# Own-row transposes of a graph-attention layer, emitted later behind their gather

## The chip, the cores and the metric

The kernel runs on one core of one Trainium2 chip. The metric is the device time of one launch in microseconds (us), the median of three runs.

## The reference

Eight batches of 2048 nodes with 256 channels pass through two graph-attention layers that share one symmetric, sparse adjacency matrix (a node has between a few and 38 neighbours, itself among them). Layer 0 is this; layer 1 has four heads, additive scores and an elu in its place:

```python
h1 = einsum('bnc,cd->bnd', inp, W1)
h2 = einsum('bnc,cd->bnd', inp, W2)
h3 = einsum('bnc,cd->bnd', inp, W3)
e = einsum('bnd,bmd->bnm', h1, h2)
e = where(adj > 0, leaky_relu(e, 0.2), NEG_INF)
h_prime = einsum('bnm,bmd->bnd', softmax(e), h3)
x = layernorm(x + relu(h_prime))
```

## The kernel before, in words

**Sparse form.** A set-up sorts the nodes by their number of neighbours and cuts them into 16 tiles of 128 rows. Each tile t has SLOTS[t] slots (38 down to 12), and a slot holds one neighbour of each of its 128 rows. A **unit** is one layer, one half of the batches (4 of 8, so a row is 1024 numbers) and one tile. Layer 0 has 32 units: half 0 with the tiles from the fewest slots to the most, then half 1 likewise. With W1 and W2 multiplied beforehand into A, a score is the product of g (own row times A) with the neighbour's raw row, so only raw rows are gathered.

**Four parts of a unit in layer 0.**
- `before0` (L503): an indirect DMA on POOL gathers the unit's own rows into xo (L505; xo has two buffers), four DMAs on SP copy them to xr for the residual (L509), TensorE transposes xo in two groups of four (L515, through `transposed`, L403), ScalarE copies each group into xT (L405), TensorE multiplies by A (L413), and ScalarE evicts the two halves into g (L520). Then the unit is marked ready.
- `logits0` (L524): VectorE multiplies every gathered row with g and sums it (L540), 4 batches a slot; then come leaky relu, mask, exp and the division by the sum.
- `sums0` (L620): ScalarE scales each gathered row by its weight in place (L631), and TensorE adds the slot to accumulators in PSUM by identity matmuls (L609, `add_slot`; the profile counts 8 matmuls a slot). The add frees the slot's ring tile.
- `after0` (L659): ScalarE evicts the sums into hs (L644), TensorE transposes hs and multiplies by W3, VectorE adds the residual and takes statistics, ScalarE normalises y (L393), TensorE transposes y into x1T and makes the projection q for layer 1 (L693), which POOL scatters to a table in HBM (L197).

**The ring.** Gathered neighbours come in chunks of two slots into a ring of 16 tiles (32 slots), shared by all units. `pump` (L461) issues a chunk's gathers as soon as a credit is there; `sums0` gives the credit back when it emits the last add of a chunk, and on the chip the gather waits until that add is done.

**What sets the order.** A driver written in Python emits everything in **ticks** (L901). In each, `sums` has just emitted one slot; then `tick` pumps gathers, lets the score stream run up to two steps while it is less than a limit ahead, and moves the first generator of each of three queues, starts (`before0`), ends (`after0`) and lists:

```python
for queue in queues:
    for _ in range(min(len(queue), 2)):
        if queue and next(queue[0], queue) is queue:
            queue.popleft()
clock[0] += 1
```

Only the head of a queue moves, so a start that takes longer holds the ones behind it. The start of unit j + 3 is queued when at most half of unit j's slots are left to add (L934); the first three units are queued at the beginning. POOL's instructions keep the order of emission (L337). The other engines' are ordered by the planner of the language, which takes emission as priority and may put a later instruction first where an earlier one isn't ready in its own estimate. `before0` counts its distance from gather to transposes with four bare `yield`s (L512). LATE is 6, and `clock[0]` is the number of the tick.

Of the kernel before, what the change touches and what calls it, by code (L numbers as in the profile page):

```python
# [40 lines left out]
LATE = 6  # L41
# [82 lines left out]
def fast_path(  # L124
# [59 lines left out]
    def wide_tile(name):  # L184
        return wp.tile([P, 2 * QW], F32, tag="t", name=name)

    def gather(dst, table, index):

        nc.gpsimd.indirect_dma_start(  # L189
            out=dst, out_offset=None, in_=table, in_offset=AT(ap=index, axis=0),  # L190
            bounds_check=table.shape[0] - 1, oob_is_err=False,
        )
# [205 lines left out]
    def transposed(src, name, dst):  # L398

        for i in range(2):  # L400
            pt = ps_tile(f"ps_t_{name}_{i}")
            for j in range(4):
                nc.tensor.transpose(pt[:, ts(j, P)], src[:, ts(4 * i + j, P)], ident)  # L403
            yield
            nc.scalar.copy(dst[:, ts(i, 512)], pt)  # L405
        yield

    def projected(srcT, weight, name, evict):
        for i in range(2):
            pp = ps_tile(f"ps_p_{name}_{i}")  # L410
            for j in range(2):
                for k in range(KC):
                    nc.tensor.matmul(  # L413
                        pp[:, ts(j, C)],
                        lhsT=srcT[:, ts((2 * i + j) * KC + k, P)],
                        rhs=weight[:, k, :],
                        start=(k == 0),
                        stop=(k == KC - 1),
                    )
            yield  # L420
            evict(i, pp)
        yield
# [23 lines left out]
    clock = [0]  # L446
# [56 lines left out]
    def before0(u):  # L503
        xo = xop.tile([P, HC], F32, tag="xo", name=f"xo_{u.name}")
        gather(xo, xg[u.h][:, :], order[:, u.t : u.t + 1])  # L505
        u.xr = xrp.tile([P, 2, HW], F32, tag="xr", name=f"xr_{u.name}")
        for r in range(2):
            for c in range(2):
                nc.sync.dma_start(  # L509
                    u.xr[64 * c : 64 * c + 64, r, :], xo[64 * r : 64 * r + 64, ts(c, HW)]  # L510
                )
        for _ in range(4):  # L512
            yield
        xT = wide_tile(f"xT_{u.name}")
        yield from transposed(xo, f"x_{u.name}", xT)  # L515
        while scored[0] < u.index - 1:
            yield
        u.g = gp.tile([P, HC], F32, tag="g", name=f"g_{u.name}")
        yield from projected(
            xT, w.A, f"g_{u.name}", lambda i, pp: nc.scalar.copy(u.g[:, ts(i, 512)], pp)  # L520
        )
        u.ready = True
# [357 lines left out]
    for j, u in enumerate(units):  # L880
        u.index = j
    before = (before0, before1)
    logits = (logits0, logits1)
    sums = (sums0, sums1)
# [354 lines left out]
```

## Time and profile before

| | us |
|---|---|
| median of three runs | 2752.31 (2752.2 to 2755.29) |
| the profiled execution's own time | 2757.27 |
| its span, first to last instruction | 2755.5 |
| busy: VectorE / TensorE / POOL / ScalarE | 2358.9 / 1884.3 / 1509.5 / 1475.2 |
| TensorE waiting for xo at the transposes (L403) | 165.1, 27 times |
| VectorE waiting for gathered chunks at L540 | 135.9 |
| first and last transposes of own rows, start | 120.5 and 1535.2 |

Layer 0 takes the span up to about 1720 us, layer 1 the rest. In the profile's rows a group is named by line, engine, operation and the tiles it writes and reads (out<-in); x and a number is a count, and what stands behind an arrow in brackets is what ended the idle time just before. A tile of the ring appears as s, a table of raw rows in HBM as xg.

### The profile page before, as it was taken

What the parts mean: (1) busy time and instruction counts of PE and PEld (TensorE: products, weight loads), DVE (VectorE), ACT (ScalarE), POOL (GpSimd) and SP (SyncE); (2) the same over time, 40 slices, a digit from 0 to 9 for tenths busy, and PEclk for the clock granted to TensorE, in tenths of its full rate; (3) what the DMA queues carried; (4) which work ended last, traced back from release to release, by engine and by line L of the source; (5) the groups of instructions that cost most, each with busy time, mean ns of one, the idle gap of its engine ahead of it and who ended that gap; (6) DMA issues with size and microseconds to landing.
All of it is one profiled execution on the core that took longest, in us unless ns stands there. A gap on an engine that the chain in (4) does not pass through costs nothing. (4 is left out here: it accounts for less than half of the span.)

```text
span 2755.5 us, 41008 instructions
## 1 busy us (share of the span) xinstructions
PE 1884.3 (68%) x12003; PEld 788.4 (29%) x12003; DVE 2358.9 (86%) x7255; ACT 1475.2 (54%) x3465; POOL 1509.5 (55%) x1506
## 2 busy tenths in 40 slices
PE   0148888888776767676878677766566576675663
PEld 0123434333333334343333322311122112121221
DVE  7679999999987875777787786799999899999996
ACT  6137777878779986868788779221111111210212
POOL 1354454545444543544544455577767777775772
PEclk9569899999898888898888888878878888877886
DMA  9996776868674665767776765799789999986991
GB/s 388 386 374 216 263 278 226 281 227 274 233 244 168 212 218 197 262 215 254 234 263 229 257 223 193 272 337 351 270 313 352 329 335 335 361 312 254 340 337 66
DMA packets 248024, 749.41 MB, mean 272 GB/s; under 512 B 55712, under 2 KB 73248, under 8 KB 241648
## 3 DMA queue, kind: packets, MB, share of 16 engines
q0 software_dynamic: 192064, 644.32, 66.2%
q1 hardware_dynamic: 54464, 101.21, 10.3%
q8 instruction: 98, 1.61, 0.2%
q10 hardware_dynamic: 1264, 1.18, 0.1%
q14 instruction: 134, 1.10, 0.1%
HBM read 721.50 MB, written 84.48 MB: 292 GB/s over the span
## 5 line engine op out<-in xcount | busy, mean ns | idle before, releaser
L609 PE MATMUL acc<-s,ident 64*64 64x512 f32 x9632 | 1363.4, 659 | 448.5 <-issue 226.6
L540 DVE CUSTOM_DVE_ANT_0 j<-s,g 128x256 bf16<-128x256 f32 x2408 | 1019.5, 423 | 201.5 <-DMA s<-xg,idx 135.9
L189 POOL DMA_INDIRECT s<-xg,idx x602 | 631.0, 1048 | 769.0 <-ACT s L631 283.5
L631 ACT ACTIVATE s<-s,e 128x256 f32<-128x256 f32 x2408 | 999.2, 503 | 27.3 <-DVE e L566 26.5
L189 POOL DMA_INDIRECT s<-qg,idx x602 | 610.6, 1014 | 249.9 <-issue 123.8
L609 PEld LDWEIGHTS acc<-s,ident 64*64 64x64 f32 x9632 | 386.5, 145 | 1219.2 <-issue 675.6
L793 DVE TENSOR_TENSOR s<-s,p 128x2048 f32<-128x2048 f32 (+1 forms) x312 | 682.0, 2201 | 0.8 <-issue 0.2
L381 ACT ACTIVATE z<-mv,roots 128x4 f32<-128x4 f32 x64 | 18.9, 296 | 509.7 <-DVE mv L371 509.6
L540 DVE DVE_READ_ACCUMULATOR2_ANT e<- 128x1 f32 x2408 | 196.0, 81 | 0.0
L693 PE MATMUL ps_q<-wqs,x1T 128*128 128x264 f32 x512 | 147.4, 425 | 37.2 <-ACT x1T L405 25.9
L197 POOL DMA_INDIRECT out_dram<-o,oidx x128 | 129.9, 1015 | 75.2 <-ACT o L393 40.1
L403 PE MATMUL ps_t_x<-ident,xo 128*128 128x128 f32 x256 | 56.6, 364 | 165.1 <-DMA xo<-xg,order 165.1
L393 ACT ACTIVATE o<-xr,nmr,rstd 128x256 f32<-128x256 f32 x128 | 66.4, 589 | 134.1 <-DVE nmr L389 102.2
L413 PE MATMUL ps_p_g<-A,xT 128*128 128x256 f32 x512 | 129.8, 400 | 9.5 <-DVE so L702 5.5
L413 PE MATMUL ps_p_h<-w_sb,hT 128*128 128x256 f32 x512 | 127.8, 392 | 1.5 <-ACT hT L405 1.5
L693 PEld LDWEIGHTS ps_q<-wqs,x1T 128*128 128x128 f32 x512 | 100.5, 206 | 88.9 <-ACT x1T L405 31.2
L413 PEld LDWEIGHTS ps_p_g<-A,xT 128*128 128x128 f32 x512 | 97.1, 197 | 53.8 <-DVE so L702 9.0
L488 DVE MAX8 m<-nb 128x8 f32<-128x2048 f32 x44 | 100.5, 2285 | 13.3 <-DMA nb<-edges,order 13.2
L413 PEld LDWEIGHTS ps_p_h<-w_sb,hT 128*128 128x128 f32 x512 | 92.1, 190 | 63.3 <-issue 19.5
L760 ACT ACTIVATE e<-e 128x304 f32<-128x304 f32 (+11 forms) x34 | 14.9, 439 | 175.7 <-DVE e L759 175.6
L403 PEld LDWEIGHTS ps_t_x<-ident,xo 128*128 128x128 f32 x256 | 37.9, 184 | 232.9 <-issue 219.0
L393 ACT ACTIVATE y<-y,nmr,rstd 128x256 f32<-128x256 f32 x128 | 67.2, 589 | 32.1 <-DVE nmr L389 31.8
(128 smaller groups left out, 1426.6 us busy)
## 6 DMA issues: line engine op xcount, KB each, us to landing
adj<-in_adj_dram SPq DMA_DIRECT2D x16, 1024.0 KB, 8.9
edges<-adj SPq DMA_DIRECT2D x16, 1024.0 KB, 19.7
xr<-xo SPq DMA_DIRECT2D x128, 128.0 KB, 6.7
x1s<-y SPq DMA_DIRECT2D x32, 512.0 KB, 7.4
xr<-x1s SPq DMA_DIRECT2D x32, 512.0 KB, 6.9
s<-xg,idx POOLq DMA_INDIRECT x602
s<-qg,idx POOLq DMA_INDIRECT x602
xg<-in_x_dram SPq DMA_DIRECT2D x4, 2048.0 KB
```

Of the source, the lines that this page charges most:

```text
L189: nc.gpsimd.indirect_dma_start(out=dst, out_offset=None, in_=table, in_offset=AT(ap=index, axis=0), bounds_check=table.shape[0] - 1, oob_i ...
L197: ins = nc.gpsimd.indirect_dma_start(out=table, out_offset=AT(ap=index, axis=0), in_=src, in_offset=None)
L381: nc.scalar.activation(z, mv[:, :, 1], AF.Ln, bias=w.roots[:, 0:1])
L393: nc.scalar.activation(dst[:, b, :], y[:, b, :], AF.Identity, bias=nmr[:, b : b + 1], scale=rstd[:, b : b + 1],)
L403: nc.tensor.transpose(pt[:, ts(j, P)], src[:, ts(4 * i + j, P)], ident)
L413: nc.tensor.matmul(pp[:, ts(j, C)], lhsT=srcT[:, ts((2 * i + j) * KC + k, P)], rhs=weight[:, k, :], start=(k == 0), stop=(k == KC - 1),)
L488: nc.vector.max(m[:, ts(i, 8)], v)
L540: nc.vector.tensor_tensor_reduce(out=jt, in0=rows[:, s, ts(b, C)], in1=u.g[:, ts(b, C)], scale=1.0, scalar=0.0, op0=ALU.mult, op1=ALU.add, ...
L609: nc.tensor.matmul(acc[r][64 * c : 64 * c + 64, :], lhsT=ident[rr, rr], rhs=rows[rr, s, c * 2 * w_ : (c + 1) * 2 * w_].rearrange("p (j w) ...
L631: nc.scalar.activation(v, v, AF.Copy, scale=u.p[i][:, b, k : k + 1])
L693: nc.tensor.matmul(pq[:, : C + 2 * H], lhsT=x1T[:, ts(i * KC + k, P)], rhs=w.wqs[:, k, :], start=(k == 0), stop=(k == KC - 1),)
L793: nc.vector.tensor_tensor(v, v, pv.unsqueeze(3).to_broadcast([P, n * HB, H, D]), ALU.mult)
```

## The change

The four bare yields between the gather of own rows and their transposes are replaced by a wait on the driver's clock: eight ticks after the gather's tick for every unit but the first, two for the first. Nothing else is edited; the gather and the copies to xr are still emitted where they were.

```diff
@@ -509,7 +509,9 @@
                 nc.sync.dma_start(
                     u.xr[64 * c : 64 * c + 64, r, :], xo[64 * r : 64 * r + 64, ts(c, HW)]
                 )
-        for _ in range(4):
+
+        then = clock[0] + (LATE + 2 if u.index else 2)
+        while clock[0] < then:
             yield
         xT = wide_tile(f"xT_{u.name}")
         yield from transposed(xo, f"x_{u.name}", xT)
```

## The prediction, made before the result was known

> **What bounds the kernel now.** Units are counted 0 to 31 in the order of layer 0 (16 tiles of half 0, then 16 of half 1); a slot is one neighbour of all 128 rows of a unit. I read the 40 slices first: VectorE stands at 7 to 9 tenths all through layer 0 but highest in its first half. So I took the engines by stage (columns: us; busy us of PE, PEld, DVE, ACT, POOL, with counts).
>
> ```profile
> 345.00:750.00 405.00, 334.79 (x1812) 146.15 (x1812) 389.41 (x1534) 321.56 (x795) 199.55 (x190) 0.93 0.74 256
> 998.00:1250.00 252.00, 181.82 (x1147) 98.67 (x1148) 177.28 (x853) 192.62 (x468) 111.97 (x106) 0.86 0.69 231
> 1250.00:1535.00 285.00, 222.90 (x1344) 106.75 (x1343) 220.80 (x1055) 224.03 (x552) 136.29 (x130) 0.86 0.72 243
> ```
>
> Units 7 to 14 (345 to 750) are VectorE's: 389.4 of 405 us, 96%. Units 19 to 30 (998 to 1535) have no full engine: VectorE 70 to 77%, ScalarE 76 to 79%. There the waits of that stretch speak (us in total, times, longest):
>
> ```profile
> PE ps_t_x L403 <- DMA xo<-xg,order: 122.1, 13, 12.2
> DVE j L540 <- DMA s<-xg,idx: 93.6, 58, 7.3
> ...
> POOL s L189 <- PE acc L609: 52.3, 19, 9.9
> ...
> ACT xT L405 <- PE ps_t_x L403: 27.1, 13, 7.8
> ```
>
> TensorE waits 13 times, 9.4 us each, for the gather of own rows, which the moved transposes read. Busy time and these waits fill its time: 181.8 + 222.9 + 122.1 = 526.8 of 537 us. One of these units, on TensorE, on POOL's queue and on ScalarE:
>
> ```profile
> 1183.62 2.00 PE L413 MATMUL ps_p_h<-w_sb,hT 128*128 128x256 f32 x8
> 1185.54 7.10 PE L609 MATMUL acc<-s,ident 64*64 64x512 f32 x64
> 1203.89 1.09 PE L403 MATMUL ps_t_x<-ident,xo 128*128 128x128 f32 x4 [11.25 <-DMA xo<-xg,order]
> 1204.91 1.99 PE L609 MATMUL acc<-s,ident 64*64 64x512 f32 x8
> 1206.83 0.68 PE L403 MATMUL ps_t_x<-ident,xo 128*128 128x128 f32 x4
> 1207.34 0.60 PE L403 MATMUL ps_t_x<-ident,y 128*128 128x128 f32 x4
> ```
> ```profile
> 1187.42 1.14 POOL L189 DMA_INDIRECT s<-xg,idx  x1 [3.42 <-issue]
> ...
> 1192.76 1.03 POOL L197 DMA_INDIRECT qg<-q,orderP  x1 [0.30 <-ACT y L393]
> 1194.10 0.97 POOL L197 DMA_INDIRECT qg<-q,orderP  x1 [0.31 <-ACT y L393]
> 1195.38 1.04 POOL L189 DMA_INDIRECT xo<-xg,order  x1 [0.30 <-issue]
> ```
> ```profile
> 1194.14 8.47 ACT L631 ACTIVATE s<-s,e 128x256 f32<-128x256 f32 x21
> 1205.02 0.58 ACT L405 COPY xT<-ps_t_x 128x512 f32<-128x512 f32 x1 [2.41 <-PE ps_t_x L403]
> ```
>
> TensorE adds eight slots in 7.1 us (0.9 each; 8 matmuls are a slot), stops at 1192.6, and stands until the gather lands at 1203.9. POOL issues that gather only at 1195.4, behind chunk gathers that wait for ring tiles which the same adds free, and behind two scatters: it lands 7.5 us after its issue ends. ScalarE goes on scaling meanwhile (5 slots) and idles only 2.4 us. So TensorE is last. Counted up to 1202 us, POOL has gathered 413 slots (438 indirect gathers from xg less 25 of own rows), VectorE scored 408, TensorE added 383:
>
> ```profile
> 0.00:1202.00 1202.00, 481.95 (x3064) 120.31 (x3064) 0.87 0.75 260
> ```
>
> 30 of the ring's 32 slots wait for TensorE, and VectorE's 93.6 us of waits for chunks are the ring being full.
>
> **What the skill says.** "TensorE: Matmul & The Clock Gate", section on the mechanism of packing, has matmuls in strict order; only weight loads are pulled ahead. The trace agrees: no add ran in the 11.25 us, though ScalarE had scaled slots ready. "DMA: Bandwidth & Descriptors", anatomy of a gpsimd DMA, gives some 2.0 us fixed plus bytes over 436 GB/s: an estimate of 3.2 us for these 0.52 MB. The trace has 7.5 us behind other gathers; the measurement is used. "Perfetto Trace Analysis", optimization strategy, asks for the gaps of the contended engine and what releases them; that is the reading above.
>
> **The change, part by part.** First, its size. A tick advances a queue by min(its length, 2) steps (L909). With one generator in starts, the four yields are four ticks, not two; with several, two. So the diff moves transposes from 4 ticks behind the gather to 8 in the steady state, and from 2 to 8 for unit 1. The trace confirms the old place: unit 24's gather is emitted after slot 379, and its transposes stand after 3064/8 = 383. Following the driver, 220 of the 256 transposes stand exactly where it emits them, although engines other than POOL are reordered by the planner. I take the new place from emission too.
>
> *Unmoved:* the gather, the four row copies on SP, and every chunk gather of the steady state keep their place; POOL and SP are not passed. *Moved with the transposes:* two ScalarE copies (0.58 us each), two projections of TensorE (1.9 us each) and two evictions into g on ScalarE (0.58 each). Following the driver, from unit 4 on the score stream first asks for g seven or more ticks after its second eviction, so four ticks fit and no score moves. In time, g is ready 12 to 50 us before its first score except in units 17 to 20 (25, 20, 0.2, 1.9); for these it is paced by the landing, which doesn't move. Even if 5 us late there, VectorE is over 20 slots ahead of the adds: cost nothing.
>
> *What fills the wait:* the TensorE work that is now ahead of the transposes. The time from a unit's transposes to the next gather's landing shrinks by just that work, since POOL's backlog and the landing hang on the same adds as before. Prices: slot 0.95 us, four transposes of y (X) 0.60, a projection q 0.95 (1.05 alone, 2.83 for three). From the driver's ticks: unit 19 passes one slot and two X, 2.2 us; 20, half a slot, two X, two q, 3.6; 21, one and a half slots, two X, one q, 3.6; 22 to 24 about three slots or two and q, with two X, 4.05 each; 25 and 26, three slots, X, two q, less a quarter slot, 5.1 each; 27 to 30, four slots, X, two q, 6.3, but capped by present waits of 5.7 and 4.8 in 27 and 30; 31, four slots and four q, 7.6. Sum 2.2+3.6+3.6+12.15+10.2+5.7+6.3+6.3+4.8+7.6 = 62.5 us, of 122.1. In 19 to 26 (31.8) I take all: ScalarE is busy 31 to 35 us of some 42, VectorE 26 to 35, so both allow it. In 27 to 31 (30.7) a unit of about 46 us would come near to VectorE's 35 to 39 and ScalarE's 36 to 43; I take 70%, 21.5. Late next there: scores and scaling.
>
> *Units 15 to 18:* waits of 5.7, 1.3, 8.6, 1.1 us, but ScalarE has 52 to 63 of each 57 to 71 us; gain 3, between 0 and 10. *Units 4 to 14:* waits of at most 5.8, under a VectorE at 96%: 0.
>
> *Start-up:* unit 1 holds the queue 6 ticks longer, so unit 2's gather goes from tick 11 to 16, past two chunk gathers, and unit 3's from 20 to 27. Unit 2's transposes then follow the last add of unit 0 (about 200 us), g some 8 us later; its scores start at 212.7. Unit 3's follow slot 22 (about 234), g near 244, scores at 247.7. Hidden by 4 us each; if not, VectorE-bound time is lost in full, up to 10. I take 1.
>
> Sum: 31.8 + 21.5 + 3 - 1 = 55 us. Profiled execution 2757.3 (span 2755.5 and 1.8 around) to 2702; it lies 5 above the median 2752.3, so 2697 for the median. Layer 1 starts from the same state, only earlier.
>
> **Rivals.** *Wait moved only in part* (gain 6 to 35, about 2730): the planner pulls the transposes forward where TensorE has nothing ready, or ScalarE and VectorE close the gap. For it: few transposes did stand off their emission. Against it: 220 of 256 didn't. Worked out: half of 55 is 27. *No change:* the wait is hidden behind another engine; then 2752. Against it, TensorE's filled time. *The wait comes back longer, slower:* q now stands ahead of the transposes, and it needs the copy of x1T, which in ScalarE's order follows long runs of scaling. Place: units 20 to 23 and 25 to 31. ScalarE reaches its copies on average 1 us before the landing (idle 27.1/13 = 2.1 us, less the 1.09 us of the transposes). If the copy is later than the landing by more than the work passed (3.6 to 6.3 us), each such unit gets longer than now: at 8 us by about 3, and 11 units give 2752 + 33 = 2785; with half the units late and the others unchanged, 2770. Against it: in the unit shown y is normalised by 1194.2 and ScalarE through its run by 1202.6, both ahead of the landing.
>
> **How the numbers follow.** Forecast (gain 35 to 85) 0.60, partial 0.23, no change 0.06, slower 0.11. Low end: all 62.5, 10 from units 15 to 18, and 12 more where ring tiles that come free earlier shorten VectorE's waits for chunks: 2668. High end: down to a gain of 10, 2742; outside lie slower, no change and the very top. A measurement tells about 0.2% (5.5 us) from no change: faster 0.83, same 0.06, slower 0.11.
>
> **What would show it.** Right: transposes of units 19 to 31 four ticks further on; TensorE's wait for xo down from 122 to about 60 us; waits of VectorE for chunks lower; 345 to 750 unchanged in length; 998 to 1535 shorter by about 50. Wrong: TensorE waiting for ScalarE at q or x1T in that stretch, g awaited by VectorE, or start-up longer by 10 us.

## The result, and the profile after

The median is 2747.15 us over 14 runs, against 2755.14 over 14 runs of the kernel before: ratio 0.997 (95% interval 0.996 to 0.998), 8 us or 0.3% less. The forecast was 55 us less, range 10 to 84: the sign was right, the size a seventh, and the time lies outside the range. By its size it falls at the lower end of the rival "wait moved only in part" (gain 6 to 35), which had a chance of 0.23. Of the two mechanisms of that rival, the planner pulling the transposes forward isn't what the profile shows; ScalarE closing the gap is near it, but was priced by halving the forecast. The profiled execution took 2751.6 us (span 2749.7).

Engines by stage, the same three stretches as before (us; busy us of PE, PEld, DVE, ACT, POOL, with counts; clock, DMA share, GB/s):

```profile
345.00:750.00 405.00, 325.83 (x1835) 147.24 (x1834) 390.36 (x1542) 324.41 (x797) 200.27 (x190) 0.92 0.75 258
998.00:1250.00 252.00, 195.05 (x1162) 103.24 (x1164) 183.62 (x872) 198.36 (x486) 113.19 (x108) 0.86 0.68 232
1250.00:1535.00 285.00, 220.09 (x1348) 102.10 (x1340) 223.42 (x1052) 219.29 (x543) 139.44 (x132) 0.90 0.72 244
```

The first stretch is as it was, VectorE at 96%. In the other two TensorE is not freed: its busy time is 415.1 us, before 404.7. Of the waits of 998 to 1535 us (total, times, longest), those that bear on the change:

```profile
...
PE ps_q L695 <- ACT x1T L405: 77.1, 11, 9.8
DVE j L542 <- DMA s<-xg,idx: 68.1, 46, 8.3
...
POOL s L189 <- PE acc L611: 19.7, 9, 9.4
...
PE ps_q L695 <- DVE so L704: 11.5, 8, 2.8
```

TensorE's wait for xo fell from 122.1 to 7.2 us (one wait, unit 24), more than forecast. In its place TensorE waits 77.1 us at q, the projection behind x1T, for a copy by ScalarE, and 11.5 more there for VectorE. In the table of costly groups that is

```profile
L695 PE MATMUL ps_q<-wqs,x1T 128*128 128x264 f32 x512 | 178.1, 489 | 156.9 <-ACT x1T L405 123.7
```

123.7 us of waiting for x1T, against 25.9 before. One of these waits, on TensorE and then on ScalarE:

```profile
1141.09 0.93 PE L403 MATMUL ps_t_x<-ident,y 128*128 128x128 f32 x4 [1.94 <-ACT y L393]
1141.95 1.13 PE L611 MATMUL acc<-s,ident 64*64 64x512 f32 x8
1143.01 1.11 PE L403 MATMUL ps_t_x<-ident,y 128*128 128x128 f32 x4
1153.40 2.13 PE L695 MATMUL ps_q<-wqs,x1T 128*128 128x264 f32 x4 [9.28 <-ACT x1T L405]
1155.32 1.06 PE L403 MATMUL ps_t_x<-ident,xo 128*128 128x128 f32 x4
```
```profile
1140.44 2.08 ACT L393 ACTIVATE y<-y,nmr,rstd 128x256 f32<-128x256 f32 x4
1142.42 10.46 ACT L633 ACTIVATE s<-s,e 128x256 f32<-128x256 f32 x26
1152.78 0.57 ACT L405 COPY x1T<-ps_t_x 128x512 f32<-128x512 f32 x1
```

The transposes of y are done by 1144.1. ScalarE's copy of them comes only after a run of 26 scalings (10.46 us), so q starts at 1153.4. The own-row transposes now stand behind q (1155.32) and find xo in place: they no longer wait, and the time is much the same.

A second account, worked out from both traces: on TensorE, the time from the start of each instruction to the start of the next, between the adds of slots 301 and 540 (units 16 to 29). What goes over 0.2 us in steps of more than 0.6 us is called *long waits*; it does not depend on the ends of matmuls, which the profile models.

| us, slots 301 to 540 | before | after |
|---|---|---|
| length | 626.0 | 625.5 |
| own-row transposes, waits included | 160 | 38 |
| q, waits included | 65 | 176 |
| all long waits | 199 | 180 |

The transposes give up 122 us, q takes 111. So the wait moved and shrank by 19 us, and short steps grew by as much: those of q by 12 us and those of the projection by A by 8, for the most part.

What moved in the order of the engines is counted in the same stretch. On TensorE, the transposes of own rows stand 2.4 slots further on, on average, and the projection by A 2.6; the transposes of hs and y, the projection by W3 and q stand where they stood. On ScalarE, the copies of x1T stand behind the same scalings as before (0.2 slots further on, on average; 22 of 27 within 0.3). So the place of q, and that of the copy that it needs, are not the change's doing: the wait at q was in the order all along, and the wait for xo, which held the transposes of y too, had covered it.

Seen along the program, by the end of each unit's adds, after minus before: unit 15 -1.7, unit 16 -18.0, unit 21 -25.5, unit 22 -15.4, unit 28 -18.0, unit 31 -6.9, end of the span -5.8 us. These are two single executions. A run below with eight ticks in half 0 alone has half 1 in the order of the kernel before, and its ends of units 15 to 31 lie within 2.5 us of that kernel's, so most of these differences are larger than the difference between one execution and another there.

### The profile page after: what moved, and what is told of

It reads as the page before. It is cut to its first block, busy times and chain, and to the rows that moved or that the text cites. A ratio compares the mean times of both kernels' runs of the same rounds, so it can differ in the third digit from the quotient of the medians.

```text
span 2749.7 us, 40978 instructions
## 1 busy us (share of the span) xinstructions
PE 1891.7 (69%) x12003; PEld 791.7 (29%) x12003; DVE 2368.8 (86%) x7255; ACT 1474.6 (54%) x3465; POOL 1514.5 (55%) x1506
## 5 line engine op out<-in xcount | busy, mean ns | idle before, releaser
L611 PE MATMUL acc<-s,ident 64*64 64x512 f32 x9632 | 1337.9, 657 | 424.7 <-issue 220.9
L611 PEld LDWEIGHTS acc<-s,ident 64*64 64x64 f32 x9632 | 380.8, 144 | 1185.7 <-issue 680.5
L695 PE MATMUL ps_q<-wqs,x1T 128*128 128x264 f32 x512 | 178.1, 489 | 156.9 <-ACT x1T L405 123.7
L695 PEld LDWEIGHTS ps_q<-wqs,x1T 128*128 128x128 f32 x512 | 110.8, 236 | 244.1 <-ACT x1T L405 144.8
L413 PE MATMUL ps_p_g<-A,xT 128*128 128x256 f32 x512 | 141.4, 422 | 9.3 <-ACT xT L405 8.4
L413 PEld LDWEIGHTS ps_p_h<-w_sb,hT 128*128 128x128 f32 x512 | 92.7, 189 | 54.2 <-issue 21.1
L562 ACT ACTIVATE e<-e 128x76 f32<-128x76 f32 (+11 forms) x34 | 8.9, 261 | 176.1 <-DVE e L561 176.1
L746 DVE TENSOR_TENSOR e<-s,own 128x32 f32<-128x32 f32 (+1 forms) x312 | 55.9, 184 | 34.8 <-DMA s<-qg,idx 34.0
L403 PE MATMUL ps_t_h<-ident,hs 128*128 128x128 f32 x256 | 50.8, 332 | 47.8 <-ACT hs L646 46.1
```

The costliest lines, as they stand in the source:

```text
L413: nc.tensor.matmul(pp[:, ts(j, C)], lhsT=srcT[:, ts((2 * i + j) * KC + k, P)], rhs=weight[:, k, :], start=(k == 0), stop=(k == KC - 1),)
L611: nc.tensor.matmul(acc[r][64 * c : 64 * c + 64, :], lhsT=ident[rr, rr], rhs=rows[rr, s, c * 2 * w_ : (c + 1) * 2 * w_].rearrange("p (j w) ...
L695: nc.tensor.matmul(pq[:, : C + 2 * H], lhsT=x1T[:, ts(i * KC + k, P)], rhs=w.wqs[:, k, :], start=(k == 0), stop=(k == KC - 1),)
L746: nc.vector.tensor_tensor(e[:, c * CHUNK : c * CHUNK + ns, :].rearrange("p s (b g) -> p s b g", b=HB), rows[:, :ns, :].rearrange("p s (b w ...
```

## The experiments

Three theories go through them. **TensorE theory**, that of the prediction: TensorE's work and its wait for xo fill its time, so a wait taken away is time gained. **ScalarE-order theory**: the next operand stands behind ScalarE's scaling, and its wait takes over. **Ring theory**: the pace is that of slots coming free in the ring. Runs were made on several chips; each ratio is to the kernel before, run beside it.

By the time of the kernel before beside them, the runs are of two kinds. The first kind, with 2755 to 2759 us, are the result, the sweep with the two runs behind it, the units in two parts and the first three under "Work left out"; the others have some 2845 us. Most of the difference lies behind layer 0: with the early gather, of the second kind, the adds of layer 0 end at 1727.7 us of 2838.8, in the kernel before at 1719.3 of 2755.5. But in slots 301 to 540 TensorE's steps from one add to the next exceed 0.6 us 48 to 69 times in runs of the second kind and 18 to 30 times in the first (the run with half the adds aside), and there is no trace of the kernel before of the second kind. So a sum of long waits is to be set against sums of its own kind; and a gain counted from the early gather's ratio, 0.9976 in the second kind, carries that ratio over where the run is of the first.

### Waits moved away

**Gather earlier, transposes where they were** (the kernel before, with)
```diff
-        for _ in range(4):
+        for _ in range(8 if u.index > 2 else 4):
...
-            if not begun and left <= u.K / 2 and j + 3 < len(units):
+            if not begun and left <= u.K / 2 + 4 and j + 3 < len(units):
```


> The kernel before, with the gather of own rows (and its copies to xr) emitted four ticks earlier from unit 3 on, while the transposes keep their old tick. TensorE theory (TensorE's time sets the units 19 to 30, so whatever wait goes shortens them): the wait for xo falls from 122 us in 998 to 1535 us to below 30, nothing takes its place, and the time falls by 40 to 60 us. ScalarE-order theory (what TensorE needs next is a copy by ScalarE that stands behind a run of 5 to 6 slots of scaling): the wait for xo falls as well, but ps_p_g then waits for xT or ps_q for x1T by 50 us or more in that stretch, and the time falls by 5 to 20 us. Ring theory (the turn of the 32 ring slots sets the pace and TensorE's wait is slack in it): time within 8 us of before.

Measured 0.9976 (0.9967 to 0.9985), 7 us less, though TensorE's wait for xo was 7.4 us: the number of the ring theory and of the ScalarE-order theory, not that of the TensorE theory. Its largest waits in 965 to 1600 us:

```profile
PE acc L609 <- ACT hs L650: 13.7, 1, 13.7
PE ps_t_h L403 <- ACT hs L644: 13.5, 4, 8.2
PE acc L609 <- issue: 13.4, 21, 1.3
```

No single one is large, and yet the long waits of slots 301 to 540 sum to 175 us, 51 of them ahead of adds (21 in the trace before, which is of the other kind). The wait was spread, not removed.

**Copies of x1T on VectorE** (the changed kernel; `transposed` given a copy, half 1 only)
```diff
-        yield from transposed(y, f"x1_{n}", x1T)
+        yield from transposed(
+            y, f"x1_{n}", x1T, nc.vector.tensor_copy if h else nc.scalar.copy
+        )
```


> The changed kernel, with the two evictions of x1T moved from ScalarE to VectorE in the second half of layer 0 (units 16 to 31), some 1.2 us of VectorE a unit. ScalarE-order theory: the 77 us in which ps_q waits for x1T in 998 to 1535 us fall below 25 and the time falls by 25 to 50 us against the changed kernel (about 2700 to 2720). Ring theory: the wait falls too, but another takes its place and the time stays within 8 us of the changed kernel. If VectorE's own queue delays the copy as ScalarE's did, the wait stays and the time rises by up to 20 us (16 units by 1.2).

Measured 0.9966 (0.9954 to 0.9978): what the change alone has, as the ring theory had it. q's wait that names the copy (965 to 1600 us) is

```profile
PE ps_q L697 <- DVE x1T L405: 28.3, 8, 9.1
```

against 83.7 us with the change alone. How much of that is the copy's place isn't shown, as that trace is of the other kind: with two credits fewer (below), the copy on ScalarE and this kind, it is 36.2. q's long waits for all causes still come to 69 us here, and all long waits to 184.

**Copies of x1T and xT on VectorE** (the same for `x_{u.name}`)

> The changed kernel, with the evictions of both x1T and xT on VectorE in units 16 to 31 (2.4 us of VectorE a unit). ScalarE-order theory: no copy that TensorE needs before its projections stands behind scaling any more; 30 to 60 us less than the changed kernel, at least as good as with x1T alone. Ring theory: within 8 us of the changed kernel, TensorE's waits found elsewhere (hs, scaled slots, y).

Measured 0.9963 (0.9953 to 0.9974); long waits 183. So ScalarE's order is not by itself what holds q: its long waits are 68 us with both copies off ScalarE.

**All three moves at once** (early gather, both copies on VectorE, and ahead of q)
```diff
+        for _ in range(4 if u.index >= 18 else 0):
+            yield
```


> The kernel with the gather four ticks earlier, and in half 1 both copies of the transposes (xT and x1T) on VectorE and q emitted four ticks later behind them: every place where TensorE was seen to wait for over 20 us in units 16 to 31 is moved away. TensorE theory in its first form (these waits are time that can be had): at least 30 us faster than before, ratio below 0.989. Wait re-forms (TensorE is fed at ScalarE's and the ring's pace, and what is taken from one wait comes back in another or in slower adds): ratio 0.993 to 0.999, as the three versions before it.

Measured 0.9955 (0.9941 to 0.9970); long waits 170. A new one is there, at the projection by A for the copy xT, now on VectorE (965 to 1600 us):

```profile
PE ps_p_g L413 <- DVE xT L405: 43.8, 12, 10.6
```

The first form of the TensorE theory falls here: the waits that it counted as time are gone from their places, and 0.45% came of it.

### Work left out

All on the kernel with the early gather, in half 1 of layer 0. Each leaves a part of the work out and serves for its time alone. In the traces, slots 301 to 540, TensorE's instructions stand among the adds where they stand in that kernel, as far as the adds are all there.

**Every second slot not added**
```diff
+        if u.layer == 0 and u.h == 1 and k % 2 == 1 and k < K - 1:
+            return
```


> The kernel of the early gather, with every second slot's add left out in units 16 to 31 (its output is then not the reference's): TensorE is spared some 8 us a unit, 130 us in all. TensorE theory: 80 to 130 us less than the early gather's 0.998 of before (ratio 0.95 to 0.97). Ring theory (a turn of the ring runs through scoring, exp, scaling, release and gather; TensorE's adds are only a short piece of it): at most 20 us less, ratio 0.990 to 0.998.

Measured 0.9633 (0.9617 to 0.9649): 95 us less than with the early gather (0.9976), for 139 slots, at 0.9 us some 125 us of TensorE's work: the number of the TensorE theory. A chunk's tile may also come free one add earlier here, so a part of this gain may be the ring's.

**One batch of four not scaled**
```diff
-                for b in range(HB):
+                for b in range(HB - u.h):
                     v = rows[:, s, ts(b, C)]
```


> The kernel of the early gather, with the scaling of one batch of four left out in units 16 to 31 (rows are added unscaled there): ScalarE is spared 0.41 us a slot, some 7.5 us a unit, 120 us in all. If ScalarE's work is a piece of the turn that nothing hides: 50 to 110 us less, ratio 0.96 to 0.98. TensorE theory: under 10 us, ratio 0.994 to 0.998.

Measured 1.0027 (1.0014 to 1.0041), no gain but some 14 us more than with the early gather, above both forecasts, and why isn't known: ScalarE idled 231 us of 626 in slots 301 to 540 in place of 137 of 622, and TensorE's long waits were 192.

**One batch of four not scored** (the same range in `logits0`, its scores set to 0)

> The kernel of the early gather, with the scores of one batch of four left out in units 16 to 31 (they are set to zero there): VectorE is spared 0.47 us a slot, some 8.8 us a unit, 140 us in all. If VectorE's scoring is a piece of the turn that nothing hides: 50 to 120 us less, ratio 0.955 to 0.98. TensorE theory: under 10 us, ratio 0.994 to 0.998.

Measured 0.9929 (0.9908 to 0.9949), 13 us less than with the early gather for some 140 us of VectorE's work, just outside the TensorE theory's forecast.

**Every second matmul of the three projections left out** (q's lines; the other two projections likewise, by a parameter)
```diff
-            for k in range(KC):
+            for k in range(KC - h):
...
-                    stop=(k == KC - 1),
+                    stop=(k == KC - 1 - h),
```


> The kernel with the gather four ticks earlier, with every second matmul of the three projections (own rows by A, sums by W3, q) left out in half 1 of layer 0; adds, scaling and scores are all there. Leaves out about 16 x 5.9 = 94 us of TensorE's work (a group of eight matmuls of a projection took 2.0 us, a q 0.95). TensorE theory (all of TensorE's work in these units counts, as leaving out 139 slots of adds, some 125 us, gave 95): a gain of some 70 us over that kernel, ratio to before 0.970 to 0.978. Ring theory, restated (what counts is only when a slot's ring tile comes free, and the adds do that; other work of TensorE lies in waits): a gain of at most 20, ratio 0.990 to 0.998.

Measured 0.9814 (0.9794 to 0.9834): 46 us less than with the early gather, for some 94 us of work. Between the two theories: work that frees no ring tile counts too, by a half. Its long waits are 198 us: they grew by 23 over the early gather's.

### The ring

**Two credits fewer** (the changed kernel, `credits = [RING - 2]`)

> The changed kernel, with 14 credits for ring tiles in place of 16 (28 slots). Ring theory: the units 16 to 31 turn slower by about 2/16, so layer 0 gets 50 to 90 us longer. ScalarE-order and TensorE theories: the ring is full only because TensorE is last, so fewer tiles cost under 20 us.

Measured 1.0175 (1.0141 to 1.0209): some 58 us more than the change, the number of the ring theory and three times what the other two allow. Fewer tiles do cost.

**One tile more, and the buffers it needs** (the changed kernel)
```diff
-RING = 16
+RING = 17
...
-    xop = ctx.enter_context(tc.tile_pool(name="xown", bufs=2))
+    xop = ctx.enter_context(tc.tile_pool(name="xown", bufs=1))
...
-    wp = ctx.enter_context(tc.tile_pool(name="wide", bufs=4))
+    wp = ctx.enter_context(tc.tile_pool(name="wide", bufs=3))
...
```


> The changed kernel with a ring of 17 tiles in place of 16 (34 slots); for the room, own rows have one buffer in place of two and the wide tiles three in place of four. To be read against the next run. Ring theory: two tiles fewer had cost 57 us, so one more gains 12 to 28 us over the same buffers with 16 tiles. TensorE theory: nothing in layer 0, at most 12 us from layer 1.

> The changed kernel with one buffer for own rows and three wide tiles, ring of 16: the comparison for the run before. Both theories: 0 to 15 us slower than the changed kernel, ratio to before 0.997 to 1.003.

Measured 1.0061 (1.0038 to 1.0085) with 17 and 1.0043 (1.0027 to 1.0060) with 16. The ring theory falls in the form that a tile more is time gained. The pair has a limit: with 16 tiles the smaller buffers alone cost some 21 us against the change, more than was expected, so what a tile more is worth was tested on a kernel that they slow. From the traces, for slots 344 to 540 on average: an add ended 8.8 us before the gather of the slot 32 further on was issued with 16 tiles, 3.6 us with 17; and a scaled slot waited 21.5 us for its add with 16, 26.4 with 17. Slots come earlier and queue before TensorE.

**Units of half 1 cut into two parts** (the changed kernel, over 16 slots)

> The changed kernel, with units of more than 16 slots in the second half of layer 0 (22 to 30) cut into two parts with a softmax each, joined as unit 31 is already. Ring theory: slots wait for half as many others before they are scaled and released, so the turn is shorter; less the joining work (some 5 us of VectorE and ScalarE a unit), 10 to 50 us less than the changed kernel, ratio 0.98 to 0.993. TensorE theory: the joining adds work and tiles, time the same or up to 30 us more.

Measured 1.0123 (1.0102 to 1.0144), some 42 us more than the change: the opposite of the ring theory's forecast, and more than the 30 that the TensorE theory allowed for the joining.

### The distance itself, swept in half 1

The changed kernel with
```diff
-        then = clock[0] + (LATE + 2 if u.index else 2)
+        then = clock[0] + (12 if u.index >= 16 else LATE + 2 if u.index else 2)
```
and 2, 4 or 16 in place of 12.

> The changed kernel with the transposes two ticks behind the gather in units 16 to 31, eight elsewhere. TensorE waits longer for xo: against the kernel before by up to 2 slots x 0.95 us in each of some 13 units, about 25 us. Path theory (the wait is on the path until the copy of x1T takes over): slower than before by 10 to 25 us, ratio 1.003 to 1.009. Slack theory (in that wait TensorE has nothing else that could set the end): within 6 us of before, 0.998 to 1.002.

> The changed kernel with four ticks, as before, in units 16 to 31, eight elsewhere: half 0 of the change alone. Path theory: equal to before, ratio 0.999 to 1.001, since the gain is half 1's. Slack theory: the same number; a ratio of 0.997, as the changed kernel's, would say that the gain came from half 0.

> The changed kernel with twelve ticks in units 16 to 31. Path theory with takeover: no more gain than with eight, and VectorE waits for g in more units, ratio 0.997 to 1.004. Slack theory: within 6 us of the changed kernel, 0.995 to 0.999.

> Sixteen ticks in units 16 to 31. If the gain goes on at the 1.8 us a tick seen from 8 to 12: ratio 0.991 to 0.993. If g, awaited by VectorE 30 us with twelve ticks already, becomes last: no more gain, ratio 0.994 to 1.003.

| ticks in units 16 to 31 | ratio (interval) | largest wait of TensorE, 965 to 1600 us | long waits, slots 301 to 540 | their length |
|---|---|---|---|---|
| 2 | 1.0060 (1.0047 to 1.0073) | xo 142.5 | 203 | 638 |
| 4 | 1.0007 (0.9997 to 1.0017) | xo 124.0 | 198 | 628 |
| 8, the change | 0.997 (0.996 to 0.998) | x1T, ScalarE, 83.7 | 180 | 625.5 |
| 12 | 0.9944 (0.9928 to 0.9960) | x1T, ScalarE, 103.3 | 162 | 607 |
| 16 | 1.0004 (0.9996 to 1.0013) | xT, ScalarE, 118.2 | 184 | 637 |

The first lines of TensorE with 2 and with 4 ticks (965 to 1600 us):

```profile
PE ps_t_x L403 <- DMA xo<-xg,order: 142.5, 13, 12.9
```
```profile
PE ps_t_x L403 <- DMA xo<-xg,order: 124.0, 13, 11.9
```

Four ticks in half 1 and eight in half 0 equal the kernel before, so all of the gain is half 1's. From 2 to 4 ticks the wait for xo falls by 18.5 us and the time by 15 (0.53%, give or take 0.16): here some four fifths of the wait is time. From 4 to 8 the wait falls by some 115 (to 8.6) and the time by 10 (0.37%, give or take 0.14). With 12 the first line of TensorE and the first two of VectorE are

```profile
PE ps_q L695 <- ACT x1T L405: 103.3, 13, 11.6
```
```profile
DVE j L542 <- DMA s<-xg,idx: 38.0, 28, 8.2
DVE j L542 <- ACT g L522: 31.8, 14, 2.9
```

TensorE waits for xo nowhere and for x1T 13 times, and the kernel has the lowest ratio of those that do all the work (0.9955 for all three moves is within its interval). Both forecasts had it slower. With 16, the bill comes on VectorE:

```profile
DVE j L542 <- ACT g L522: 102.7, 23, 9.6
DVE j L542 <- DMA s<-xg,idx: 16.5, 10, 5.6
```

g is late for its scores, and the gain is gone, as the second forecast had it.

**Twelve ticks, and the copy of x1T on VectorE**

> Twelve ticks in units 16 to 31 (alone: ratio 0.9944), and there the copy of x1T on VectorE. Takeover theory (q's wait for ScalarE's copy, 103 us, is what the path now holds): 25 to 80 us less than with twelve ticks alone, ratio 0.966 to 0.985. Wait re-forms: within 7 us of it, 0.992 to 0.997, with a wait of like size at another of TensorE's operands or at the same one.

Measured 0.9964 (0.9950 to 0.9977), no better than twelve ticks alone. TensorE's wait at q is of the same size and names the other engine:

```profile
PE ps_q L697 <- DVE x1T L405: 110.8, 13, 12.3
```

**Less scaling where the waits are moved** (all three moves, one batch of four not scaled in half 1)

> The kernel with early gather, copies xT and x1T on VectorE and q four ticks later (ratio 0.9955), with the scaling of one batch of four left out in half 1: some 300 scalings of 0.4 us, 120 us of ScalarE's work. If ScalarE's scaling feeds the adds and so sets the pace once the waits are moved: a gain of 30 us or more on that kernel, ratio below 0.985. If it doesn't: within 8 us of it, 0.993 to 0.999.

Measured 0.9978 (0.9970 to 0.9987), no gain on 0.9955. ScalarE's amount of scaling doesn't set the pace there either; the wait for xT on VectorE is 80 us in slots 301 to 540.

## Why the prediction was right in sign and wrong in size

**Right.** Half 0 and start-up: the stretch 345 to 750 is as before, and unit 3 ends its adds 1.9 us earlier; forecast 0 and 1 us lost. The transposes did move on in TensorE's order (unit 24's stand behind the adds of slot 386 now, behind those of slot 383 before). The wait for xo went, VectorE's wait for chunks fell (93.6 to 68.1 us), and POOL's gathers wait less for adds (52.3 to 19.7). TensorE's work does count in units 16 to 31: a half to three quarters of what was left out came back as time, of ScalarE's nothing, of VectorE's a tenth. And between two and four ticks the wait for xo was worth four fifths of its length, as the sum takes it to be.

**Wrong: the step "What fills the wait".** It let the time from a unit's transposes to the next landing shrink by "just that work" which they pass, 62.5 us, of which 53.3 was taken. That presumes that TensorE, once past xo, finds its next operands ready. It didn't: q stood ahead in the new order, and x1T's copy came about when xo used to land, so that TensorE waited 77.1 us for x1T in place of 122.1 for xo. That ScalarE was busy for 31 to 35 us of some 42 was taken to allow the gain; but a share of busy time doesn't tell when a copy comes. Over units 16 to 29 in the profile after, the first copy of x1T starts in all 134.7 us after its transposes ended, and ScalarE is busy for 107.1 of them, nearly all with scaling that stands ahead of it. "TensorE waiting for ScalarE at q or x1T" was the prediction's own sign of being wrong. It also had the number in its hand. In the rival "the wait comes back longer" it worked out that ScalarE reaches its copies on average 1 us before the landing, and asked only whether the copy is later than the landing by more than the work passed, that is, whether the change becomes slower. A copy that comes *with* the landing, neither early nor late, has the wait re-form at nearly the old length, and that case was never worked out: "partial" took half of the forecast's gain, "no change" named another cover. The case against the rival, one unit in which y was normalised by 1194.2 and ScalarE through its run by 1202.6, showed this very thing: 1202.6 is 1.3 us ahead of the landing at 1203.9.

By terms, from the ends of adds in the two profiles. The prediction counts a term by the unit whose own rows are transposed; these transposes stand among the adds of the unit three before it (unit 19's behind slot 312, in unit 16).

| term: own rows of units | at the adds of units | gain forecast, us | measured |
|---|---|---|---|
| start-up and up to 14 | 0 to 11 | -1 | 3.8 |
| 15 to 18 | 12 to 15 | 3 | -2.1 |
| 19 | 16 | 2.2 | 16.3 |
| 20 and 21 | 17 and 18 | 7.2 | 6.9 |
| 22 to 24 | 19 to 21 | 12.2 | 0.6 |
| 25 and 26 | 22 and 23 | 10.2 | -8.9 |
| 27 to 31 | 24 to 28 | 21.5 | 1.4 |
| none left | 29 to 31 | 0 | -11.1 |

From unit 22's own rows on the terms failed, 43.9 us of the 53.3. In unit 22's adds two waits meet, the one for xo that is left (7.2 us) and one at q (7.7). The right sign was in large part luck: it rests on the adds of unit 16. There the wait for xo of 7.7 us fell to 1.4, where the forecast took 2.2 off, and a wait shrank that the prediction didn't have: the first add waits until ScalarE has emptied the accumulators of unit 15. It was 14.1 us in the kernel before, and in the sweep it is 16.4, 14.6, 8.7, 6.7 and 1.4 us with 2, 4, 8, 12 and 16 ticks; why is open. Without the 16.3 us of unit 16 the sum of the terms is a loss. How much of what was lost later is this early gain given back isn't known.

**The deeper error** is the sum: "Busy time and these waits fill its time", and from it "So TensorE is last". Such a sum comes out in every version: in slots 301 to 540 the long waits are 199 us before, from 162 to 203 in 16 further kernels, 198 with fewer credits and 217 with units in two parts, wherever they stand (with half the adds slots can't be counted so). A sum that always fills the time doesn't tell which engine is last. Nor did the ring's count: of the 30 slots that were gathered and not added at 1202 us, the prediction has all wait for TensorE. ScalarE's scalings up to then are

```profile
0.00:1202.00 1202.00, 651.67 (x1577) 0.87 0.75 260
```

and 1577/4 is 394 slots: 11 of the 30 were scaled and waited for their add, the others for scores, softmax or scaling. "TensorE: Matmul & The Clock Gate" of the Trainium skill, section on the mechanism, says that matmuls run in strict order; the trace of after agrees, as no add ran in the 9.28 us at q. A scaled slot waited 21.1 us for its add before (slots 344 to 540), 20.2 after: before, 98% of the length of the long waits has the next slot already scaled, after 94%. So there was nearly always an add that could have run, and another instruction ahead of it in the order. "Perfetto Trace Analysis", optimization strategy, sends the reader to the gaps of the contended engine and their releasers. That was done; what no list of releasers tells is which operand ends next if this one comes at once.

**What stays open.** What fixes the sum of the waits isn't settled. ScalarE's place in x1T's copy (three runs), the amount of its scaling (two runs), and the wait for xo (the sweep) are each excluded as the one cause. The ring's depth is not: two credits fewer cost 58 us, and that one tile more gains nothing rests on one pair with smaller buffers. My reading, argued and not shown: a unit's end goes to and fro between TensorE and the two engines that copy and normalise, in one common order with the next unit's scores and scaling, so each operand comes when its engine gets to that point of the order, not when its input is there. For x1T's copy the traces bear this out on both engines: with twelve ticks and the copy on VectorE, the first copies start 151.1 us in all after their transposes (units 16 to 29), and VectorE is busy for 119.9 of them, nearly all with scores that stand ahead. That this is also what holds the time isn't shown. With twelve ticks and the copy on ScalarE, ScalarE idled 4.16 us for the softmax, scaled 11 times and only then copied x1T:

```profile
1369.84 0.27 ACT L562 ACTIVATE e<-e 128x76 f32<-128x76 f32 x1 [4.16 <-DVE e L561]
1370.89 4.49 ACT L633 ACTIVATE s<-s,e 128x256 f32<-128x256 f32 x11 [0.78 <-DMA s<-xg,idx]
1375.29 0.56 ACT L405 COPY x1T<-ps_t_x 128x512 f32<-128x512 f32 x1
```
```profile
1368.04 0.66 PE L403 MATMUL ps_t_x<-ident,y 128*128 128x128 f32 x4
1368.62 1.95 PE L611 MATMUL acc<-s,ident 64*64 64x512 f32 x16
1375.91 2.12 PE L695 MATMUL ps_q<-wqs,x1T 128*128 128x264 f32 x4 [5.34 <-ACT x1T L405]
```

An order in which those copies go ahead of scores and scaling was not tried.

## What to carry to other kernels

Where an engine took its work in order, as TensorE here, removing a wait was worth at most the distance to the next operand's arrival, and often less: before pricing its removal, find for each instruction behind it when its own operand came, in the order of the engine that makes it and not from that engine's busy share, and cap the gain there. Test a bound by leaving work out, not by reading waits: here TensorE's work counted by a half to three quarters, while 115 us of its waits for xo, moved away, were worth 10. Sweep a distance rather than move it once: 2, 4, 8, 12 and 16 ticks showed the slope, its end, and the next bound.

## What the runs showed that was not expected

TensorE's long waits stayed within 162 to 203 us over seventeen kernels, while their place moved from xo to x1T, xT or to nothing that stands out; the sum isn't constant, and in the sweep the fastest kernel has the lowest. With twelve ticks, taking x1T's copy off ScalarE changed only the name of the releaser (103.3 us to ScalarE, 110.8 to VectorE). And a deeper ring lengthened the queue before TensorE by the 5 us that it had taken from the gathers' wait.
